# Three rows of an expert pair side by side for each partition

## The chip, the cores and the metric

The kernel runs on one core of a Trainium2 chip. The metric is the device time of one execution in microseconds; a kernel is judged by the median of several runs. The engines of the core are TensorE (PE), VectorE (DVE), ScalarE (ACT), GpSimd (POOL) and SyncE (SP, which here only issues DMAs). Each works through its own instructions in the order in which they stand, and waits on semaphores where an instruction needs another engine's or a DMA's result.

## The reference, cut to what matters

Four blocks of attention and feed-forward are applied to 4 x 256 tokens of width 256. Only the last feed-forward matters for the change: a mixture of 64 experts, of which each token takes eight. Its router and experts compute

```python
h = layernorm(x)                                  # 1024 tokens, width 256
logits = h @ gate_w                               # 64 experts
w, e = top_8(softmax(logits))                     # eight choices a token, weights summing to 1
y[token] = sum_j w[token, j] * ((silu(h @ gate_proj[e_j]) * (h @ up_proj[e_j])) @ down_proj[e_j])
x = x + y                                         # inner width of an expert: 96
```

## The kernel before

**The layers before the experts** are written as generators (`layers`, from line 450). Each step yields an `Op` with its engine, a cost in us, and what it reads and writes; a small planner (`Flow.run`) picks at every moment the request that can start first by these declared costs, with a due time as a tie-breaker, and so fixes the order of the instructions on each engine at build time. The costs that a step declares thus move the steps of other threads, too. There are two versions of the layers, for two kinds of token ids; this input takes the one built with `nk = 1`.

**Tiles.** The 1024 tokens are eight tiles of 128, one token a partition. `tile3` (line 1611) ends the last attention for one tile. Its `ps_y` (line 1623, PE) is the output projection; `add_to_x` (line 927, DVE) adds it to the tile's x. What `ps_y` needs is made by `heads3` (line 1594): exponentials on ACT (line 1566), transposes `tp_e` on PE (line 1588) with copies on ACT (line 1590), products `ps_u` on PE (line 1604) with copies to `u` on ACT (line 1608). Then the tile is routed: logits `ps_l` on PE (line 1644), the eight best on DVE (lines 1646 to 1648), and `ps_pos` on PE (line 1652), which counts for each token and expert how many tokens before it chose that expert. From this count, `pos`, DVE makes the place of each choice (lines 1657 to 1663) in `slots`.

**Places.** Each expert has room for `CAP = 192` rows; `hs` in HBM has 64 x 192 rows of 257 words: 256 of the normalized token, and one with the number of the row of `yd` to which the result belongs. Expert e's row number `pos` lies at 192 e + pos. The table `first` holds 12288 - 192 e; `first - pos` is taken so that the largest value is the first place, `ok` is 0 where the expert is full or not chosen.

**Scatter.** `normed_rows` (line 1671) makes eight copies of a tile's normalized rows in `hx`: POOL raises the variance to its power (line 1684), ACT writes the copies in two activations (line 1689). `scatter` (line 1696) sends one choice j of a tile at a time to `hs`: an indirect DMA that POOL issues (line 1702), 64 in all.

**Loads of rows.** `fill_rows` (line 441) loads the 384 rows of a pair of experts into a tile of 128 partitions x 3 x 257 words. Row number r of the pair goes to partition r mod 128, block j = r div 128, so each of the 384 runs is 1028 bytes long. SP issues these loads (line 443); the first three are issued in the layers. A load waits for the puts that can hold rows of its pair: pair 0 for choices 0 and 1 of all tiles, pair 1 for choices 0 to 3, pair 3 and later ones for all.

**Experts.** `experts` (line 2040) goes through 32 pairs in an order written out by hand. `rows_turned` (line 1887) transposes the six 128x128 blocks of a pair (`tp_hb`, PE), ACT copies them to `hbT`; then gate and up products (`ps_gu` line 2055, `ps_u` line 1986), their product on DVE (lines 1991 and 2071), and the down products `ps_y` (lines 1999 and 2004). ACT copies `ps_y` over the pair's rows (line 2083), and `put_results` (line 2007) scatters the three blocks j = 0, 2, 1 to `yd` by the row numbers in word 257. `beside` issues later loads: rows seven pairs ahead, weights, and from pair to pair the finished results of a choice (line 1927). At the end `sums` adds the weighted results to x and stores.

In the columns of `hbT`, block j and partition p stand at column 128 j + p; the first expert of a pair owns columns 0 to 191, the second 192 to 383.

Of the kernel before, what the change touches and what calls it, by code (L numbers as in the profile page):

```python
# [23 lines left out]
I32 = mybir.dt.int32  # L24
AF = mybir.ActivationFunctionType
ALU = mybir.AluOpType
AX = mybir.AxisListType

P = 128
# [17 lines left out]
E3, I3, K3 = 64, 96, 8  # L47
# [9 lines left out]
CAP = 192  # L57
HALF = P // 2
RPP = 2 * CAP // P
NROWS = E3 * CAP  # L60
# [12 lines left out]
PE, DVE, ACT, POOL, SP = "PE", "DVE", "ACT", "POOL", "SP"  # L73
# [43 lines left out]
class Flow:  # L117
# [22 lines left out]
    def go(self, gen, due=0.0):  # L140
        th = Thread(gen, due)
        self.threads.append(th)
        self.resume(th, None)
        return th
# [10 lines left out]
    def release(self, *bufs):  # L155

        for b in bufs:
            self.roles[b.role][b.slot] = max(b.used, b.ready or 0.0)
# [76 lines left out]
def model(ctx: ExitStack, tc: tile.TileContext, a: dict, out: bass.AP):  # L235
    nc = tc.nc
    PSUM = bass.MemoryType.PSUM

    const = ctx.enter_context(tc.tile_pool(name="const", bufs=1))
# [8 lines left out]
    def scal(n, name):  # L248
        return small.tile([P, n], F32, tag=f"s{n}", name=name)

    def held(pool, shape, name, dtype=F32):
        return pool.tile(shape, dtype, tag=name, name=name)
# [4 lines left out]
    def x_t(t):  # L257
        return xb[t // 2][:, t % 2, :]
# [20 lines left out]
    hs = dram.tile([NROWS, HW], F32, tag="hs", name="hs")  # L279
# [43 lines left out]
        channel_multiplier=-1,  # L323
    )
    onesb = held(const, [P, P], "onesb", BF16)
    nc.gpsimd.memset(onesb, 1.0)
    first_i = held(const, [P, E3], "first_i", I32)
    nc.gpsimd.iota(first_i, pattern=[[-CAP, E3]], base=NROWS, channel_multiplier=0)
    first = held(const, [P, E3], "first")
    nc.vector.tensor_copy(first, first_i)  # L330
    sel = held(const, [P, NT, E3], "sel", BF16)
    lgs = q1_both.rearrange("p k i -> p (k i)")[:, 2 * RPP * HW : 2 * RPP * HW + 2 * NT * E3]
    lgs = lgs.bitcast(F32).rearrange("p (t e) -> p t e", t=NT)
# [32 lines left out]
    ps = banks.tile([P, 2, NT], F32, tag="bank0", name="ps_far")  # L366
# [54 lines left out]
    def needs(ld, group, wanted, reason):  # L421

        for w in wanted:
            tc.add_manual_dep(
                ld.ins, w.name,
                mybir.DependencyInfo(mybir.DependencyClass.Sync, mybir.DependencyReason.DATA),
                reason=reason,
            )
        tc.declare_no_dep(ld.ins, group=group, keep=wanted + readers, reason=reason)
        tc.add_to_no_dep_group(group, ld.ins)  # L430
        readers.append(ld.ins)

    hbs = {
        p: v[:, : 2 * RPP * HW].bitcast(F32).rearrange("p (j d) -> p j d", j=RPP)
        for p, v in enumerate(
            (q2[2], q1_both.rearrange("p k i -> p (k i)"), q12, wmask.rearrange("p t s -> p (t s)"))
        )
    }
    in_early = len(hbs)

    def fill_rows(p, since):

        ld = nc.sync.dma_start(
            hbs[p], hs[2 * p * CAP : 2 * (p + 1) * CAP, :].rearrange("(j p) d -> p j d", p=P)
        )
        wanted = [i for n, js in zip(since, puts[: 2 * p + 2]) for i in js[n:]]
        needs(ld, "put", wanted, "rows of these choices alone")
        tc.add_to_no_dep_group("rows", ld.ins)

    def layers(nk):  # L450
# [4 lines left out]
        def due(b, stage):  # L455
            return DUE[stage] + SKEW * b
# [26 lines left out]
        def bank(shape, name):  # L483
            return ("bank", shape, name)

        def a2(shape, name, dtype=F32):
            return ("a2", shape, name, dtype)

        def a4(shape, name):
            return ("a4", shape, name)  # L490
# [17 lines left out]
        SEL = [Buf() for _ in range(NT)]  # L508
# [416 lines left out]
        def add_to_x(t, y, ps):  # L925
            yield Op(DVE, 0.39, (ps,), (X[t],))
            nc.vector.tensor_add(x_t(t), y, x_t(t))
# [428 lines left out]
        def first_rows():  # L1356
            for p in range(in_early - 1):
                yield Op(SP, 0.06, PUT[2 * p : 2 * p + 2], kb=386)
                fill_rows(p, before)
# [234 lines left out]
        def heads3(t, m, q, u):  # L1594


            n, b, es = 4 // nk, t // 2, [None, None]
            first = m * n // 4 * 8 + m * n % 4
            at = due(b, "h3") + 15.0 * (t % 2) + 3.0 * n / 2 * m
            yield Join([go(softmax3(t, first + 4 * i, q, es, i), at + 3.0 * i) for i in range(2)])  # L1600
            o = yield Op(PE, 1.25, (*es, KEYS3[b]), new=[bank([P, n, P], "ps_u3")])
            for kc in range(nk):
                for r, e in zip((lower, upper), es):
                    nc.tensor.matmul(
                        o[r], kvc[:, 2 * b + kc, :], e[:, :, kc, :], start=kc == 0, stop=kc == nk - 1
                    )
            yield Op(ACT, 0.1 + 0.4 / nk, (o,), (u,))
            nc.scalar.copy(u[:, m * n : (m + 1) * n, :], o.ap)  # L1608
            release(o, *es)

        def tile3(t, q, lane, left):

            bo3 = loads["bo3"].ap[:, : H3 // 2 * D].rearrange("p (h e) -> p h e", h=H3 // 2)
            u = yield Op(None, 0.0, new=[a4([P, H3 // 2, P], "u")])
            yield Join([go(heads3(t, m, q, u), due(t // 2, "h3")) for m in range(H3 // 8 * nk)])
            at = due(t // 2, "t3") + 15.0 * (t % 2)
            yield at
            left[0] -= 1
            if not left[0]:
                release(*q, lane)  # L1620
            y = yield Op(PE, 3.5, (u, BO3), new=[bank([P, D], "ps_y")])
            for hp in range(H3 // 2):
                nc.tensor.matmul(  # L1623
                    y.ap, u[:, hp, :], bo3[:, hp, :], start=hp == 0, stop=hp == H3 // 2 - 1
                )
            yield from add_to_x(t, y.ap, y)
            release(y, u)
            hx, w = yield Op(None, 0.0, new=[("hx", "hx"), a2([P, 2 * D], "w")])
            rows = hx.ap.rearrange("p (j d) -> p j d", j=K3)
            row_data = [Buf(), Buf()]  # L1630


            go(normed_rows(t, hx, rows, row_data), at)
            hT, rest = w[:, :D].rearrange("p (c r) -> p c r", c=2), w[:, D : D + E3]
            ok, v, top = w[:, D + E3 : D + 2 * E3], order[:, t, :], tops[:, t, :]
            tp = yield Op(PE, 0.27, (X[t],), new=[bank([P, 2, P], "tp_h")])
            for dc in range(2):
                nc.tensor.transpose(tp.ap[:, dc, :], x_t(t)[:, dc * P : (dc + 1) * P], ident)
            yield Op(ACT, 0.32, (tp,), (w,))
            nc.scalar.copy(hT, tp.ap)  # L1640
            release(tp)
            lps = yield Op(PE, 0.45, (w, GATE3C), new=[bank([P, E3], "ps_l")])
            for dc in range(2):
                nc.tensor.matmul(lps.ap, hT[:, dc, :], gate3[:, dc, :], start=dc == 0, stop=dc == 1)
            yield Op(DVE, 0.75, (lps,), (SEL[t],))
            nc.vector.max(top[:, :K3], lps.ap)
            nc.vector.match_replace(rest, top[:, :K3], lps.ap, -3.0e38)
            nc.vector.tensor_tensor(sel[:, t, :], rest, lps.ap, ALU.not_equal)

            ps = yield Op(PE, 0.06 * (t + 1), SEL[: t + 1], new=[bank([P, E3], "ps_pos")])  # L1650
            for u in range(t + 1):
                nc.tensor.matmul(
                    ps.ap, onesb if u < t else tri, sel[:, u, :], start=u == 0, stop=u == t
                )
            pos, places = ps.ap, Buf()
            yield Op(DVE, 0.85, (ps, SEL[t]), (places,))
            nc.vector.scalar_tensor_tensor(ok, pos, float(CAP), sel[:, t, :], ALU.is_lt, ALU.mult)

            nc.vector.tensor_sub(v, first, pos)
            nc.vector.tensor_mul(v, v, ok)  # L1660
            nc.vector.max(top[:, K3:], v)
            nc.vector.tensor_scalar(
                slots[:, t, :], top[:, K3:], -1.0, float(NROWS), ALU.mult, ALU.add
            )
            release(ps)
            go(scatter(t, hx, rows, row_data, places, at + 100.0), at + 100.0)
            yield Op(ACT, 0.2, (lps,), (w,))
            nc.scalar.copy(lgs[:, t, :], lps.ap)
            release(lps, w)
# [56 lines left out]
        with tc.manual_schedule(engines=ORDERED | {mybir.EngineType.SP}):  # L1726
# [5 lines left out]
            w = DUE_WEIGHTS  # L1732
# [29 lines left out]
    def ps_acc(shape, name):  # L1762
        return psum.tile(shape, F32, tag="acc", name=name, bufs=2)
# [42 lines left out]
    with tc.manual_schedule(engines=ORDERED):  # L1806
# [4 lines left out]
        ps = ps_acc([P, NT], "ps_over")  # L1811
# [14 lines left out]
    with tc.If(rv > 0):  # L1826
# [13 lines left out]
        with tc.For_i(0, E3, 1) as e:  # L1840
# [4 lines left out]
            for c in range(NCH):  # L1845
# [10 lines left out]
                for k in range(TPC):  # L1856
                    t = c * TPC + k
                    y = ps_acc([P, D], "ps_y")
                    nc.tensor.matmul(y, g[:, k * P : (k + 1) * P], dn, start=True, stop=True)
                    w = scal(1, "w_left")  # L1860
# [100 lines left out]
    rest = (slice(P, CAP), slice(0, HALF))  # L1961
# [251 lines left out]
```

## Time and profile before

| What | Value |
|---|---|
| median of 8 runs | 642.53 us (640.48 to 643.85) |
| profiled execution | 641.7 us |
| its span, first to last instruction | 639.3 us |
| mean granted TensorE clock | 0.976 |
| PE busy | 587.0 us (92%) |
| DVE, ACT, POOL busy | 423.4, 373.5, 403.7 us |
| DMA packets | 66304, 98.12 MB |
| loads of rows (line 443) | 32, 385.5 KB each |
| scatter to hs (line 1702), mean of one | 1026 ns |
| scatter to yd (line 2009), mean of one | 1001 ns |

A row of the profile names an engine, a line of the kernel and an operation; `out<-in` are the program's tiles. In brackets stands how long the engine had been idle before it and what ended that. Times of rows are us from the start of the span. The busy time of PE is modelled, and some records can be missing.

### The profile page before, as it was taken

The numbers are of one execution on the slowest core, as the hardware profiler recorded it, in microseconds if no ns is written. First come the engines' busy times: TensorE is split into PE (matmuls) and PEld (weight loads), VectorE is DVE, ScalarE is ACT, GpSimd is POOL, SyncE is SP. The second block draws the span as 40 slices with busy tenths as digits, with TensorE's granted clock in tenths as the row PEclk, the third lists the DMA queues.
The fourth block names the chain that finished last, engine by engine and source line by source line (L and its number), as shares of the span: only waits on it lengthen the run. The fifth ranks groups of instructions, "written<-read, shape, count | busy, mean of one in ns | idle before, by whom it ended". The sixth has DMA issues, their size and how long they took to land. (4 is left out here: it accounts for less than half of the span.)

```text
span 639.3 us, 10891 instructions
## 1 busy us (share of the span) xinstructions
PE 587.0 (92%) x3727; PEld 448.2 (70%) x3740; DVE 423.4 (66%) x1063; ACT 373.5 (58%) x900; POOL 403.7 (63%) x532
## 2 busy tenths in 40 slices
PE   5997799998999999999999989999739999999995
PEld 4774357686688777877876866886527887788773
DVE  5679947777687779659988767475534555434437
ACT  2233337868988976456786778579444544445420
POOL 6998898122627553564735886787773777676670
PEclk9998989998999999999999999999959999999999
DMA  8999999520200023000003111053458978978688
GB/s 297 364 387 253 219 223 252 171 58 15 83 33 3 1 67 116 2 0 1 1 2 99 42 67 58 34 190 109 158 161 265 307 238 276 302 232 305 218 261 269
DMA packets 66304, 98.12 MB, mean 153 GB/s; under 512 B 7206, under 2 KB 54007, under 8 KB 66240
## 3 DMA queue, kind: packets, MB, share of 16 engines
q1 hardware_dynamic: 56320, 78.40, 41.8%
q0 software_dynamic: 7680, 16.84, 7.4%
q10 hardware_dynamic: 2240, 2.10, 1.0%
q8 instruction: 31, 0.51, 0.4%
q14 instruction: 33, 0.27, 0.1%
HBM read 58.42 MB, written 43.07 MB: 159 GB/s over the span
## 5 line engine op out<-in xcount | busy, mean ns | idle before, releaser
L2009 POOL DMA_INDIRECT yd<-hb x84 | 84.1, 1001 | 34.2 <-issue 20.4
L1702 POOL DMA_INDIRECT hs<-hx,slots x64 | 65.7, 1026 | 24.3 <-issue 12.9
L903 POOL TENSOR_TENSOR st<-st,mhalf 128x1 f32<-128x1 f32 x56 | 32.9, 591 | 57.4 <-DVE st L899 43.1
L1566 ACT ACTIVATE e<-ps_s,nm 128x128 f32<-128x128 f32 x128 | 45.9, 421 | 5.7 <-DVE nm L1560 5.6
L1991 DVE TENSOR_TENSOR act<-ps_u,g 64x192 f32<-64x192 f32 x64 | 22.7, 354 | 39.5 <-PE ps_u L1986 39.1
L2083 ACT COPY hb<-ps_y 128x768 f32<-128x768 f32 x27 | 21.6, 800 | 36.5 <-PE ps_y L2004 36.5
L2071 DVE TENSOR_TENSOR act<-ps_gu,g 32x384 f32<-32x384 f32 x32 | 18.0, 561 | 34.2 <-ACT g L2059 33.9
L1478 POOL TENSOR_TENSOR hh<-g,v 128x512 f32<-128x512 f32 x16 | 20.2, 1274 | 23.8 <-ACT g L1476 20.0
L1281 ACT ACTIVATE qT<-tp_q,rnd 128x512 bf16<-128x512 f32 (+2 forms) x48 | 25.7, 567 | 12.2 <-PE tp_q L1277 12.2
L1566 ACT ACTIVATION_READ_ACCUMULATOR e<-ps_s,nm 128x1 f32 x128 | 32.3, 260 | 0.0
L1533 POOL TENSOR_TENSOR deep<-rt 64x512 f32<-64x512 f32 x20 | 27.1, 1355 | 5.6 <-DVE rt L1529 2.7
L1519 PE MATMUL ps_q<-qc,deep 96*128 96x256 f32 x128 | 30.4, 380 | 0.0
L906 DVE TENSOR_SCALAR h<-x,st 128x256 f32<-128x256 f32 x56 | 26.7, 489 | 5.1 <-POOL st L903 4.8
L1185 ACT ACTIVATE e<-ps_s,nb 128x256 f32<-128x256 f32 x64 | 30.1, 493 | 0.0
L1623 PE MATMUL ps_y<-bo,u 128*128 128x256 f32 x128 | 29.3, 381 | 0.1
L2059 ACT ACTIVATE g<-ps_gu 96x384 f32<-96x384 f32 x32 | 15.6, 486 | 23.2 <-PE ps_gu L2055 23.2
L1900 ACT COPY hbT<-tp_hb 128x768 f32<-128x768 f32 x31 | 24.7, 798 | 7.1 <-PE tp_hb L1892 7.1
L1120 PE MATMUL ps_g<-hT,w_gate 128*128 128x512 bf16 x69 | 20.1, 431 | 7.7 <-ACT hT L1100 4.3
L1529 DVE TENSOR_TENSOR rt<-ps_q,rope 128x512 f32<-128x512 f32 x32 | 20.9, 684 | 9.4 <-PE ps_q L1519 9.4
L1583 DVE TENSOR_TENSOR e<-e,nm 128x512 f32<-128x512 f32 x32 | 25.8, 806 | 1.3
L1519 PEld LDWEIGHTS ps_q<-qc,deep 96*128 96x128 f32 x128 | 24.1, 190 | 3.5 <-ACT qc L1505 0.3
L1623 PEld LDWEIGHTS ps_y<-bo,u 128*128 128x128 f32 x128 | 23.6, 190 | 3.4 <-ACT u L1608 0.5
(373 smaller groups left out, 1773.0 us busy)
## 6 DMA issues: line engine op xcount, KB each, us to landing
hs<-order SPq DMA_DIRECT2D x1, 12336.0 KB, 86.3
hb<-hs SPq DMA_DIRECT2D x28, 385.5 KB, 5.2
yd<-order SPq DMA_DIRECT2D x1, 8192.0 KB, 29.5
deep<-in_w_gu SPq DMA_DIRECT2D x8, 768.0 KB, 7.0
wt<-in_w_gu SPq DMA_DIRECT2D x6, 768.0 KB, 5.7
deep<-in_w_dn SPq DMA_DIRECT2D x8, 384.0 KB, 6.3
wt<-yd SPq DMA_DIRECT2D x3, 1024.0 KB, 5.5
wt<-in_w_dn SPq DMA_DIRECT2D x6, 384.0 KB, 10.5
```

Of the source, the lines that this page charges most:

```text
L903: nc.gpsimd.tensor_tensor(s[:, 8:9], s[:, 7:8], mhalf, ALU.pow)
L906: nc.vector.tensor_scalar(h[:, k, :], x_t(t), ss[k][:, 6:7], ss[k][:, 8:9], ALU.subtract, ALU.mult)
L1185: nc.scalar.activation(e[:, mt, :], s[:, mt, :], AF.Exp, bias=nb[:, mt : mt + 1], accum_out=tot[:, 2 * j + mt : 2 * j + mt + 1],)
L1281: nc.scalar.activation(qT[:, 4 * i : 4 * i + full, :], tp.ap[:, :full, :], AF.Identity, bias=rnd[:, 1:2])
L1519: nc.tensor.matmul(ps.ap[:, k, :], w[:, hp * P : (hp + 1) * P], qc.ap, start=True, stop=True)
L1533: nc.gpsimd.tensor_add(qv(q[i])[r, hps, :], t0[r], t1[r])
L1566: nc.scalar.activation(wide[:, k, :], s.ap[:, k, :], AF.Exp, bias=nm[:, k : k + 1], accum_out=tot[:, k : k + 1],)
L1583: nc.vector.tensor_mul(wide, wide, tot.unsqueeze(2).to_broadcast([P, n, nk * P]))
L1623: nc.tensor.matmul(y.ap, u[:, hp, :], bo3[:, hp, :], start=hp == 0, stop=hp == H3 // 2 - 1)
L1702: put = nc.gpsimd.indirect_dma_start(out=hs[:, :], out_offset=bass.IndirectOffsetOnAxis(ap=slots[:, t, j : j + 1], axis=0), in_=rows[:, j, ...
L1900: copied = nc.scalar.copy(hbT, tp[:, :, : RPP * P])
L2009: put = nc.gpsimd.indirect_dma_start(out=yd[:, :], out_offset=bass.IndirectOffsetOnAxis(ap=hbs[p][:, j, D : D + 1].bitcast(I32), axis=0), ...
```

## The change

A pair's rows are placed differently. For position `pos` of a token in its expert, the first expert of a pair takes row 3 pos of the pair, the second row 3 pos + 2; a position from 128 on is bent back to the middle rows: the first expert's 128 to 191 go to rows 1, 4, ..., the second's to the middle rows of partitions 64 to 127. Partition p then holds rows 3p, 3p + 1 and 3p + 2, which lie side by side in `hs`, so a load is 128 runs of 3084 bytes. The columns of `hbT` belong to the same experts as before. In block j = 1, which before held the first 64 rows of the second expert and the first expert's rows past 128, now only rows past 128 of either expert lie; block j = 2 holds the second expert's first 128.

The table `first` gets a second half, `back_to`, made by a second iota and one wider cast. Two DVE operations are added for each tile, and the step declares 1.1 us in place of 0.85, and that it writes the tile's scratch `w`.

```diff
-    first_i = held(const, [P, E3], "first_i", I32)
-    nc.gpsimd.iota(first_i, pattern=[[-CAP, E3]], base=NROWS, channel_multiplier=0)
-    first = held(const, [P, E3], "first")
-    nc.vector.tensor_copy(first, first_i)
+    first_i = held(const, [P, 2, E3], "first_i", I32)
+    nc.gpsimd.iota(
+        first_i[:, 0, :], pattern=[[-2 * CAP, E3 // 2], [1 - RPP, 2]], base=NROWS, channel_multiplier=0
+    )
+    nc.gpsimd.iota(
+        first_i[:, 1, :], pattern=[[0, E3 // 2], [2 - RPP * HALF, 2]], base=RPP * P - 1,
+        channel_multiplier=0,
+    )
+    firsts = held(const, [P, 2, E3], "first")
+    nc.vector.tensor_copy(firsts, first_i)
+    first, back_to = firsts[:, 0, :], firsts[:, 1, :]
...
-            hbs[p], hs[2 * p * CAP : 2 * (p + 1) * CAP, :].rearrange("(j p) d -> p j d", p=P)
+            hbs[p], hs[2 * p * CAP : 2 * (p + 1) * CAP, :].rearrange("(p j) d -> p j d", p=P)
...
-            yield Op(DVE, 0.85, (ps, SEL[t]), (places,))
+            yield Op(DVE, 1.1, (ps, SEL[t]), (places, w))
             nc.vector.scalar_tensor_tensor(ok, pos, float(CAP), sel[:, t, :], ALU.is_lt, ALU.mult)
 
-            nc.vector.tensor_sub(v, first, pos)
+            nc.vector.scalar_tensor_tensor(rest, pos, float(P), back_to, ALU.is_ge, ALU.mult)
+            nc.vector.scalar_tensor_tensor(v, pos, float(-RPP), first, ALU.mult, ALU.add)
+            nc.vector.tensor_add(v, v, rest)
             nc.vector.tensor_mul(v, v, ok)
```

The order of the instructions before the experts changes with it on PE, DVE, ACT and POOL, from the routing of the first tile on; the orders of SP and of the expert stage are the same as before.

## Prediction

> **What bounds the kernel now.** I read the table of stages first, because the page's shares (PE 92% busy) mix stages with different limits. Its columns are start:end, length, then busy us (and instructions) of PE, PE's weight loads, DVE, ACT and POOL, then granted clock, DMA share, GB/s.
>
> ```profile
> 405.00:425.00 20.00, 20.00 (x135) 17.64 (x134) 13.86 (x37) 11.56 (x36) 15.39 (x20) 1.00 0.21 71
> 460.00:470.00 10.00, 1.61 (x14) 1.27 (x14) 3.71 (x15) 3.49 (x8) 8.13 (x18) 0.64 0.26 88
> 470.00:476.00 6.00, 1.59 (x7) 1.22 (x7) 2.75 (x7) 2.24 (x4) 5.02 (x10) 0.50 0.68 167
> 476.00:484.00 8.00, 6.78 (x34) 5.42 (x35) 1.73 (x4) 2.64 (x4) 2.02 (x3) 0.76 0.56 164
> 484.00:612.00 128.00, 128.00 (x903) 101.81 (x900) 60.62 (x146) 62.83 (x91) 88.69 (x88) 1.00 0.83 272
> 622.00:640.00 18.00, 9.95 (x38) 6.20 (x36) 13.18 (x32) 0.00 (x0) 0.36 (x2) 1.00 0.79 266
> ```
>
> The reader is to see that the expert stage (484 to 612) has PE busy for all of its 128 us, while the layers before it keep PE nearly full, and that only the passage between them, 460 to 484, leaves PE idle. There POOL is the busy engine, with the last scatters. So a row load that lands sooner is worth something in the passage and nothing inside the expert stage. The chain of waits names POOL there, but POOL only follows PE's 4.25 us per pair (its puts begin at 491.94, 496.19 and so on).
>
> Second, who waits for the row loads of line 443, asked by source line (time and count; then landing in us, least, median, most):
>
> ```profile
>   PE tp_hb L1892: 6.9, 2
>   PEld tp_hb L1892: 0.7, 1
> ...
> DMA to landing us min/median/max: 3.2/5.2/14.8
> ```
>
> Of 32 loads only the first two are waited for: 14.8 us in flight hurts nobody, since loads are issued seven pairs ahead.
>
> Third, the passage in order of time:
>
> ```profile
> 461.82 0.59 POOL L1684 TENSOR_TENSOR rstds<-st,mhalf 128x1 f32<-128x1 f32 x1
> 467.20 0.97 POOL L1702 DMA_INDIRECT hs<-hx,slots  x1 [0.22 <-issue]
> 469.89 6.04 SPq L443 DMA_DIRECT2D q<-hs  x3
> 473.84 1.51 PE L1892 MATMUL tp_hb<-ident,q 128*128 128x128 f32 x6 [6.53 <-DMA q<-hs]
> 480.45 0.87 PE L1892 MATMUL tp_hb<-ident,q 128*128 128x128 f32 x6 [0.33 <-DMA q<-hs]
> ```
>
> The last tile's scale is made at 461.82; four puts follow at 1.28 us each, the fourth (tile 7, choice 1, at 467.20) ends what pair 0 waits for; its load goes out at 469.89, is used at 473.84, and the second pair's transposes wait 0.33 us more for their load.
>
> **The change part by part.**
>
> *Two added DVE operations per tile.* The operations at lines 1657 and 1659 take 217 to 226 and 209 to 213 ns and start up to 0.26 us apart; 16 more make 16 x 0.26 = 4.2 us of DVE over 350 to 463. DVE is busy 13.86 of 20 us there, so the sum is hidden; on a path lies only the last tile's 0.5 us. It is covered too: before, that tile's slots end at 463.24 (463.07 + 0.17), and its first put starts at 465.93, behind two puts of tile 6. Cover 2.7 us, cost 0; 0.5 us if the cover is gone. The second iota and the longer cast run in the first 6 us (186 ns each before): 0, at most 0.4.
>
> *The planner's order.* The declared 1.1 in place of 0.85 us and the added write of w move instructions on PE, ACT, DVE and POOL from tile 0's slots on; on SP nothing moves. I followed the end of both orders. What decides is the time from tile 6's update of x to tile 7's:
>
> ```profile
> 451.60 0.42 DVE L927 TENSOR_TENSOR x<-ps_y,x 128x256 f32<-128x256 f32 x1 [0.29 <-PE ps_y L1623]
> 453.94 2.37 ACT L1689 ACTIVATE hx<-x,st,rstds 128x1024 f32<-128x1024 f32 x2 [0.37 <-POOL tick L1701]
> 456.32 0.58 ACT L1608 COPY u<-ps_u 128x512 f32<-128x512 f32 x1
> 458.98 0.42 DVE L927 TENSOR_TENSOR x<-ps_y,x 128x256 f32<-128x256 f32 x1 [2.85 <-PE ps_y L1623]
> ```
>
> Before, 7.38 us (451.60 to 458.98): ACT makes both copies of tp_e (452.09 and 452.99) ahead of the hx pair, so PE's last ps_u runs at 453.59 and ps_y of tile 7 at 454.85. In the new order the hx pair stands ahead of both copies, and ps_u waits for them: 2.34 (451.60 to the hx pair's start) + 2.37 (the pair) + 1.07 (two copies, 0.49 apart, the second 0.58) + 1.08 (ps_u, row at 438.12; 1.11 at 453.59) + 3.62 (a ps_y undisturbed, row at 447.94) = 10.48. That is 3.1 later, counted from tile 6. Against it, one ps_u pass (1.08) that stood ahead of tile 6's ps_y now stands behind it, so tile 6 may be up to 1.08 earlier if PE sets that stretch, and not at all if ACT does, as between 425 and 440 (14.69 of 15 us busy). I take half: 0.5. Net **+2.6** at tile 7. POOL passes it on: two puts of tile 6 and two of tile 7 stand between the scale and what pair 0 waits for, in both orders (choices 4 and 5 of tile 6 before, 5 and 6 after). Behind them come seven puts instead of eight; that 1.28 us is off the path, as pair 3's rows land at 485.96 and are used at 487.71. The whole order since 350 us is shuffled, with PE waits of only about 5 us there in all, so this term may be anything from -1.1 to +5.
>
> *The row loads.* 384 runs of 1028 bytes become 128 of 3084. The trace's packet records have 1028-byte packets at a mean of 80 ns in the first load, 64 in the next two and 58 in 520 to 560 (median 47); the nearest long ones, 512 packets of 3072 bytes at the start, at 128 (median 124). In the DMA view of 469.9 to 474.1:
>
> ```profile
> q1 hardware_dynamic: 400, 0.39, 46.2%
> q0 software_dynamic: 166, 0.49, 30.8%
> ```
>
> The first load's packets fill 384 x 80 / 16 = 1.93 us of sixteen queues, and would fill 128 x 128 / 16 = 1.02: 0.9 us sooner. By medians it is 384 x 47 / 16 = 1.13 against 0.99, so 0.1. The rest of its 3.95 us until use is latency. The second load must also come sooner to keep the gain, and it was used 0.33 us late already. I take **-0.6**, between 0 and -0.9; the value lies nearer the first because the same two streams, puts and loads, meet here again. In the expert stage each load frees (384 x 58 - 128 x 128) / 16 = 0.37 us of DMA time per 4.25 us pair: 0, hidden behind PE's 128 of 128 us; without that cover it would still be no more than 32 x 0.37 = 12.
>
> [...]
>
> *The scatters and the results.* Still 64 puts into hs (mean 1026 ns) and 96 into yd (1001 ns), with the same number of live rows; POOL's time did not depend on how many rows were live (0.97 in nearly every row), so 0. The wait for the last put changes a little: choice block j=1, put last, held 64 rows of the odd expert and now holds the overflow past row 128 alone.
>
> ```profile
> 621.31 3.58 DMA yd<-hb
> 625.93 7.47 DMA ctxT<-yd
> ```
>
> An unloaded put lands in 2.4 us (row at 606.78) against 3.58 + 0.12 here, but the put ahead of it, at 620.03, now carries more rows, and the four 512 KB loads behind fill the queues (share 0.79 over the tail). I take **-0.3**, between 0 and -1.3.
>
> **Sum.** +2.6 - 0.6 - 0.3 = +1.7. The profiled execution took 641.7 (span 639.3 and 2.4 around it), so 643.4; it lies 0.8 below the median of 642.53, so the median goes to **644.2**. About 0.2%, or 1.3 us, is what measurement can tell from no change.
>
> **Rivals.**
> *The order pays off.* Tile 6 takes the full 1.08, and enough of the hx pair's wait falls on work that PE has anyway that tile 7 is also 1.1 early. Then -1.1 - 0.9 - 0.3 = -2.3: 640.2. For it: PE waited only 3.0 us for ACT's copies at line 1590 between 340 and 460, and both orders hold the same work. Against it: the ACT order above is fixed, in-order and counted. It decides once tile 7's update comes at least 0.4 us early (-0.4 - 0.6 - 0.3 = -1.3). Chance 0.27.
> *Even.* The order costs about 1 us and the loads and tail return it: 642.6. Chance 0.22.
> *No help from longer runs.* Landing is latency and one slow queue (the second and third loads' last packets trail to 481.2), the order costs its full 3.1 and the slots' 0.5 is uncovered: +3.6, 646.1. Chance 0.15.
> *The change not doing what it says* is unlikely: the compiled loads read 128x771 in place of 128x3x257. It would be the case above.
> My forecast, slower by 1.3 to 3, keeps 0.36. So faster 0.27, same 0.22, slower 0.36 + 0.15 = 0.51. The range, **640.6 to 647.2**, takes in the first rival nearly to its value and the last with 1 us of shuffle beyond it. Slower alone would be 643.8 to 647.2.
>
> **What would show it.** Right: packets fall by 32 x 256 = 8192 from 66304; PE stays at 128 of 128 us in the expert stage; tile 7's update comes over 9 us after tile 6's, the last scale at about 464.4, pair 0's load out near 472.5, its transposes near 475.8. Wrong: a last scale at or before 461.8 (the order term), a first load not landing sooner than 3.9 us after issue (the load term), or an expert stage with a period other than 4.25 us.

## The result and the profile after

The changed kernel takes 648.70 us (median of 17 runs, 646.77 to 650.76) against 642.64 us for the kernel before on the same chip (46 runs): ratio 1.0099, 95% interval 1.0087 to 1.0111, so 6.1 us slower. The forecast was 644.2 with a range to 647.2: the right side, but outside the range. The profiled execution of the changed kernel took 650.47 us (span 648.7), 1.8 above its median, where that of before was 0.9 below its own; so the two profiles differ by 8.8 us where the medians differ by 6.1. This matters for the tail, below.

The table of stages again (start:end, length; busy us of PE, PE's weight loads, DVE, ACT and POOL; granted clock, DMA share, GB/s), with the stages about 7 us later:

```profile
405.00:425.00 20.00, 17.63 (x110) 14.37 (x109) 15.48 (x29) 11.57 (x51) 14.75 (x17) 1.00 0.36 125
467.00:477.00 10.00, 2.05 (x16) 1.47 (x16) 5.07 (x20) 3.92 (x8) 7.60 (x15) 0.67 0.26 86
477.00:483.00 6.00, 1.91 (x7) 1.54 (x8) 2.96 (x7) 2.19 (x3) 4.83 (x10) 0.50 0.68 175
491.00:619.00 128.00, 128.00 (x902) 101.62 (x902) 60.87 (x146) 62.58 (x91) 88.69 (x88) 1.00 0.81 268
629.00:648.00 19.00, 12.04 (x37) 8.19 (x35) 13.22 (x32) 0.00 (x0) 0.09 (x2) 0.82 0.76 263
```

The expert stage is as it was: PE busy for 128 of 128 us, a pair every 4.25 us. What is new stands ahead of it: from 405 to 425 PE now stands idle for 2.4 of 20 us, where it was full. The passage in order of time shows the same chain as before, later:

```profile
468.39 0.57 POOL L1693 TENSOR_TENSOR rstds<-st,mhalf 128x1 f32<-128x1 f32 x1 [0.73 <-DVE st L1690]
474.97 1.32 POOL L1711 DMA_INDIRECT hs<-hx,slots  x1 [0.23 <-issue]
476.98 5.55 SPq L450 DMA_DIRECT2D q<-hs  x3
480.52 1.51 PE L1901 MATMUL tp_hb<-ident,q 128*128 128x128 f32 x6 [4.96 <-DMA q<-hs]
486.94 1.13 PE L1901 MATMUL tp_hb<-ident,q 128*128 128x128 f32 x6
```

The last scale is 6.6 us later (468.39 for 461.82), pair 0's load 7.1 (476.98 for 469.89), its first use 6.7 (480.52 for 473.84); the second pair no longer waits for its load. From issue to use the first load takes 3.54 us where it took 3.95. The loads by source line, and the transfers while the first load is under way:

```profile
  PE tp_hb L1901: 5.0, 1
...
DMA to landing us min/median/max: 2.8/4.9/14.9
```

```profile
q1 hardware_dynamic: 144, 0.39, 42.1%
q0 software_dynamic: 173, 0.47, 30.3%
```

Packets fall from 66304 to 58112, by the 8192 forecast, and 400 packets of q1 become 144. But their time on the queues hardly falls (42.1% of a window of 4.2 us, for 46.2%). Last, the stretch from tile 6's update of x to tile 7's:

```profile
455.31 0.42 DVE L934 TENSOR_TENSOR x<-ps_y,x 128x256 f32<-128x256 f32 x1
457.65 2.37 ACT L1698 ACTIVATE hx<-x,st,rstds 128x1024 f32<-128x1024 f32 x2 [0.44 <-POOL tick L1710]
459.93 1.04 ACT L1597 COPY e<-tp_e 128x512 f32<-128x512 f32 x2
460.55 2.45 PE L1611 MATMUL ps_u<-e,kvc 128*64 128x512 f32 x4 [1.46 <-ACT e L1597]
462.93 4.04 PE L1630 MATMUL ps_y<-bo,u 128*128 128x256 f32 x16
467.01 0.42 DVE L934 TENSOR_TENSOR x<-ps_y,x 128x256 f32<-128x256 f32 x1 [6.40 <-PE ps_y L1630]
```

It is as the forecast read it off the two orders, the hx pair ahead of the copies and ps_u waiting for them, but 11.7 us long (10.48 forecast, 7.38 before); and tile 6 itself comes at 455.31, 3.7 us later than before, where the forecast had it 0.5 sooner. Together tile 7 is 8.0 us late. How PE spent the time from 340 us, where both kernels still have the same order and the changed one is 0.4 us late in this execution, to the updates of tile 6 and of tile 7; first before, then after, with one stretch more:

```profile
340.00:451.60 111.60, 106.48 (x649) 84.57 (x648) 74.46 (x194) 82.97 (x277) 83.57 (x135) 1.00 0.28 92
340.00:459.00 119.00, 113.57 (x688) 89.18 (x686) 77.39 (x207) 87.36 (x284) 88.59 (x145) 1.00 0.30 98
```

```profile
340.00:455.30 115.30, 106.81 (x648) 84.23 (x649) 78.11 (x206) 83.16 (x277) 85.16 (x138) 1.00 0.29 98
340.00:467.00 127.00, 116.22 (x691) 89.92 (x690) 81.39 (x221) 88.04 (x285) 91.94 (x153) 0.99 0.28 95
460.55:462.93 2.38, 2.38 (x5) 0.58 (x5) 0.05 (x1) 0.54 (x2) 1.35 (x3) 0.50 0.00 0
```

Idle time of PE is length less busy: 5.4 us before, 10.8 after. So of the 8.0 us, 5.35 are idle time and 2.65 are busy time. By tile 6's update the idle time is 8.5 us for 5.1: 3.4 of the 3.7 us that tile 6 is late. It was added between 380 and 437 us (5.0 us for 1.2), though tile 5's update at the end of that stretch is still on time (438.19 for 438.43). Behind tile 6 the clock plays a part: it was 0.50 from 460.55 to 462.93, while ps_u ran, and stood at 1.00 there before (453 to 459). The last ps_u took 2.45 us for 1.11 before, the last ps_y 4.04 us for the 3.62 of an undisturbed one. In the waits of PE from 340 us on no single one stands out, before and then after (total, times, longest):

```profile
PE ps_u L1604 <- ACT e L1590: 3.0, 2, 2.2
PE ps_qc L1500 <- ACT hT L922: 1.0, 2, 0.7
```

```profile
PE ps_u L1611 <- ACT e L1597: 4.9, 4, 1.6
PE tp_e L1595 <- DVE e L1590: 2.2, 4, 1.1
PE ps_pos L1659 <- DVE sel L1655: 1.0, 2, 0.8
```

### The profile page after: what moved, and what is told of

It is laid out like the page before. It is cut to its first block, busy times and chain, and to the rows that moved or that the text cites. A ratio compares the mean times of both kernels' runs of the same rounds, so it can differ in the third digit from the quotient of the medians.

```text
span 648.7 us, 10911 instructions
## 1 busy us (share of the span) xinstructions
PE 592.3 (91%) x3727; PEld 451.1 (70%) x3740; DVE 428.8 (66%) x1079; ACT 373.9 (58%) x900; POOL 404.4 (62%) x533
## 2 busy tenths in 40 slices
DMA packets 58112, 98.12 MB, mean 151 GB/s; under 512 B 7206, under 2 KB 41719, under 8 KB 58048
## 4 chain that ended last, share of the span: by engine, by line
PE 45%; POOL 14%; DVE 12%; ACT 12%; issue 11%; DMA 5%; POOLq 1%; DVEq 0%; ACTq 0%; SPq 0%
POOL yd L2018 10%; PE ps_q L1526 6%; PE ps_g L1127 3%; ACT e L1573 2%; PE ps_y L1630 2%; DMA yd<-hb 2%; PE ps_u L1127 2%; PE ps_y L1409 2%; PE tp_q L1284 2%; PE ps_u L1611 2%; PE ps_s L1387 2%; PE ps_p L749 2%; ACT hx L1698 1%; PE ps_p L945 1%; PE tp_e L1200 1%
## 5 line engine op out<-in xcount | busy, mean ns | idle before, releaser
L1711 POOL DMA_INDIRECT hs<-hx,slots x64 | 65.1, 1018 | 25.4 <-issue 11.5
L910 POOL TENSOR_TENSOR st<-st,mhalf 128x1 f32<-128x1 f32 x56 | 32.8, 590 | 57.0 <-DVE st L906 44.8
```

What stands on the lines that cost most here:

```text
L910: nc.gpsimd.tensor_tensor(s[:, 8:9], s[:, 7:8], mhalf, ALU.pow)
L1711: put = nc.gpsimd.indirect_dma_start(out=hs[:, :], out_offset=bass.IndirectOffsetOnAxis(ap=slots[:, t, j : j + 1], axis=0), in_=rows[:, j, ...
```

## The experiments

Theory: the time comes from the order that the planner writes out for the new declaration. Rivals: the added operations or the new layout cost it; or, within the order, one place alone (tile 6's hx pair). The kernels ran in five groups, each on one chip beside the kernel before. In the first three groups that kernel took 682.0, 674.6 and 682.7 us, in the last two 642.9 and 642.1; so only ratios to the kernel before within a group are compared, and moments only within a group, or between the last two groups and the first measurement.

### First group: which part of the change

The four corners: layout old or new, declaration old or new, and the declaration's two halves.

```diff
 e1, in the changed kernel:
-            yield Op(DVE, 1.1, (ps, SEL[t]), (places, w))
+            yield Op(DVE, 0.85, (ps, SEL[t]), (places,))
 e2, in the kernel before:
-            yield Op(DVE, 0.85, (ps, SEL[t]), (places,))
+            yield Op(DVE, 1.1, (ps, SEL[t]), (places, w))
 e3, in the changed kernel: Op(DVE, 1.1, (ps, SEL[t]), (places,))
 e4, in the changed kernel: Op(DVE, 0.85, (ps, SEL[t]), (places, w))
```

> The changed kernel with the routing step declared as before (0.85 us, without the write of w): same instruction order as before, new places, new loads and the two added DVE operations kept. Theory 'order' (the loss is the planner's new order; it measured +8.0 us at the last tile's update of x): tile 7's update comes within 1 us of 459.0, pair 0's transposes start at about 473.3 (the shorter load gives 0.4 back), and the time is 641.5 to 643, equal to before within 0.2%. Theory 'layout' (the two operations and the new places cost it): still 646 or more.

> The kernel before with only the declaration changed (1.1 us and the write of w): the changed kernel's instruction order, with the old places, the 1028-byte runs and no added operation. Theory 'order': slower by 5.5 to 7.5 us, 648 to 650, tile 7's update at 466 to 467. Theory 'layout': equal to before within 0.2%.

> The changed kernel with 1.1 us declared, but without the write of w: a third order. Theory 'order' in the form that any shuffle of an order costs: slower than before by 2 to 8 us. In the form that only this one order is bad (the hx pair ahead of two copies on ACT, near its end): within 2 us of before, and the distance from tile 6's to tile 7's update of x says which: 7.4 us where the copies go first, over 10 where they do not. Theory 'layout': 646 or more whatever the order.

> The changed kernel with 0.85 us declared and the write of w: a fourth order. Theory 'order': its time follows tile 7's update of x one for one (time = 642.5 + that update's time - 459.0, within 1.5 us), whatever its sign. Theory 'layout': 646 or more whatever the order.

Measured, as ratio to before with its 95% interval: e1 1.0006 (0.9977 to 1.0034), e2 1.0070 (1.0031 to 1.0108), e3 1.0102 (1.0047 to 1.0156), e4 1.0035 (1.0009 to 1.0061). With the old declaration the new layout and the added operations cost nothing that can be measured here; with the new declaration the old layout is slower by 0.7%, which its interval does not tell from the changed kernel's 1.0%. In the profiles e2's tile 7 is 8.6 us later than e1's (486.0 for 477.4) and its first transposes 7.0 (500.0 for 493.0), and its span is 6.9 longer. The order is the cause. Each half of the declaration gives another order: e3's time can't be told from e2's, and e4's lies between e1's and theirs, with an interval that overlaps both. The rule that e4 was to test, the time following tile 7's update one for one, did not hold: e4's tile 7 is 4.3 us after e1's and its median 1.7, e2's 8.6 and 5.2.

### Second group: which order, and which place in it

```diff
 e5, in the changed kernel, ahead of the hx activations:
+            if t == 6:
+                yield due(3, "t3") + 40.0
 e6: Op(DVE, 0.95, (ps, SEL[t]), (places,))
 e7: Op(DVE, 1.0, (ps, SEL[t]), (places, w))
 e8: e1 again
```

> The changed kernel, with one exchange on ACT and nothing else moved on PE, DVE or POOL in the branch that runs: the two hx activations of tile 6 stand behind the two copies of tp_e again. Theory 'one stretch' (the forecast's: the added time comes from the stretch between the x updates of tiles 6 and 7, where ps_u waits for the hx pair): tile 7's update comes 2.4 us sooner, the two updates stand 9.3 us apart, the time is 646.3 us, 1.006 of the kernel before. Theory 'many gaps' (PE stands still a little in some ten places of 340 to 467, and this is one of them): tile 7's update gains no more than the gap at this place, 1.46 us, the two stand 10.2 us apart or more, the time is 647.2 or later, at or above 1.0073, and the remaining 5 to 6 us stay.

> The changed kernel with 0.95 us declared for the slots on DVE in place of 1.1 (with or without the write of w the order comes out the same): the planner writes out a third order. Theory 'any other order costs' (the order of before is a lucky one, and the order that follows from any other declared cost leaves PE more idle): PE's idle time between 340 us and tile 7's update is above 8 us against 5.4 before, and the time is 1.004 of before or more. Rival 'the 1.1 order is a bad one by itself': a cost close to the old one gives a time within 0.3% of before. Rival 'the layout or the two operations cost': it stays at 1.007 or more whatever the order.

> The changed kernel with 1.0 us declared and the write of w kept: a fourth order. Theory 'any other order costs': 1.004 of before or more, with more than 8 us of PE idle between 340 us and tile 7's update. Rival 'the 1.1 order is a bad one by itself': within 0.3% of before, or faster. In both, the end follows the first transposes of the expert stage by about 165.5 to 168 us, so the time can be read off the moment of the first tp_hb.

> The changed layout and the added operations in the old order (0.85 us declared, places alone written), once more, beside the kernels with other orders and with five rounds, to bound what layout and operations do by themselves. By the forecast's terms: loads -0.6, tail -0.3, operations 0, so 0.9986 of before (-0.9 us). By 'the tail pays' (in the changed kernel's profile the last transposes stand 34.5 us from the end, before 31.8): +0.9 to +2.7 us, 1.0015 to 1.004. By 'operations cost 0.5 at the last tile': 0 to +0.5 with the loads' gain, 1.000.

(What e6 says in brackets does not hold: with the write of w the order at 0.95 is another, which was not run. In e5 the pair came to stand between the two copies, not behind both.)

Measured: e5 1.0102 (1.0066 to 1.0138), e6 0.9996 (0.9971 to 1.0021), e7 1.0018 (0.9991 to 1.0044), e8 1.0028 (1.0004 to 1.0053). So it is not so that any other order costs: those of 0.95 and 1.0 measure within 0.2% of the kernel before, and their first transposes come at 489.1 and 489.8, where e8 has 489.4 and e5 496.1. The orders of 1.1 us are bad by themselves. (From the first transposes to the end it is 183.6 to 185.4 us in these four, not the 165.5 to 168 that e7 names.) e8 is the kernel of e1, which measured 1.0006 on another chip; here its interval lies just above 1, where "the tail pays" had it, so a cost of layout and operations of up to 0.5% on this chip is not excluded. In e5 the two updates stand 10.0 us apart, but tile 6 comes at 472.1, 5.7 us later than in e8: most of the loss stands ahead of the place that the forecast named. Its interval is too wide to say whether the exchange gave back 1.5 us.

### Third group: early or late tiles, and an order that seemed better

```diff
 e9 and e10, in the changed kernel:
-            yield Op(DVE, 1.1, (ps, SEL[t]), (places, w))
+            new = t < 4          # e10: t >= 2
+            yield Op(DVE, 1.1 if new else 0.85, (ps, SEL[t]), (places, w) if new else (places,))
 e11, in the kernel before: Op(DVE, 0.95, (ps, SEL[t]), (places,))
 e12: e6 again
```

> The changed kernel with the new declaration (1.1 us and the write of w) for the slots of tiles 0 to 3 alone, the old one for tiles 4 to 7: in the branch that runs, PE, DVE and POOL keep exactly the changed kernel's order, ACT differs in a few copies. Theory 'upstream' (the loss is made by PE's order from about 350 us on, which the first tiles' declaration sets, and tile 6 is late already): the time is 1.007 to 1.010 of before, and tile 6's update of x comes 3 us or more later than in the old order on the same chip. Forecast's theory (tile 6's own hx pair ahead of the copies, tile 6 no later): tile 6 within 1 us of the old order, and the loss, if any, all behind it.

> The changed kernel with the new declaration for tiles 2 to 7 alone, the old one for tiles 0 and 1: PE and DVE keep exactly the old order, on ACT only the small copies of ps_l stand one or two places elsewhere. Theory 'upstream': 1.000 of before, at most 1.003. Rival 'the price of the late tiles' slots counts' (a wait for w or a later place that the longer declaration asks for by itself): 1.004 or more.

> The kernel before, old layout and no added operations, with 0.95 us declared: the order on PE and ACT is that of the changed layout with 0.95 us (the next kernel), so the two differ in layout and added operations alone. Theory 'order': within 0.3% of before, as the changed layout was with this order. Rival 'old layout gains by this order what the new one then loses': 0.997 of before or less.

> The changed layout and operations with 0.95 us declared, beside the old layout in the same order on the same chip. By the forecast's terms (loads -0.6, tail -0.3, operations 0) 0.9 us less than its neighbour; the load of pair 0 is used 0.4 to 0.6 us sooner after its issue. By 'the tail pays': 1 to 3 us more than its neighbour, and seen between the last transposes and the end. By 'the operations cost 0.5 at the last tile': 0 to 0.5 more.

Measured: e9 1.0076 (1.0034 to 1.0118), e10 0.9982 (0.9957 to 1.0006), e11 0.9946 (0.9923 to 0.9968), e12 0.9992 (0.9969 to 1.0014). With the new declaration for the first tiles alone PE's order is the changed kernel's, the time can't be told from it, and tile 6 is at 476.9 where e10, with PE's old order, has 466.5. With the new declaration for tiles 2 to 7 PE's order stays, and so does the time. "Upstream" stood the test; the price of the late tiles did not. The pair e11 and e12 was a surprise: one order, yet the new layout 3.2 us slower, and e11 faster than before. Hence the next group.

### Fourth group: operations and layout by themselves

```diff
 e13: e11 again
 e14: e11 with
+            nc.vector.scalar_tensor_tensor(rest, pos, float(P), first, ALU.is_ge, ALU.mult)
             nc.vector.tensor_sub(v, first, pos)
+            nc.vector.tensor_add(rest, v, rest)
 e15: e6 again
```

> The old layout with 0.95 us declared, on another chip, beside the next two, which have its order exactly on PE and ACT. Theory 'this order is better than the old one': 0.9946 of before again, at most 0.998. Rival 'no better, the 3.7 us belonged to that chip': 0.998 to 1.002.

> The kernel of e13 with the two added DVE operations of the same shapes (64 columns, one of them read from PSUM), their result used by nothing: old layout, same order, so the difference to e13 is the price of the operations alone. Forecast: 0 (cover 2.7 us at the last tile), at most 0.5 us. Rival 'the operations cost': 8 tiles of about 0.4 to 0.5 us on the way from ps_pos to the scatters, 1 to 3 us if they push the puts of every tile.

> The changed layout with its operations in the same order: the difference to e14 is the price of the layout alone, scatter places and loads. Forecast: -0.9 us. Rival 'the layout costs' (on the chip of e11 and e12 layout and operations cost 3.2 us together, seen between the first transposes and the end): +1 to +3 us here too, seen there again. If e13 to e15 are within 1.5 us of one another, the 3.2 us were that chip's or chance.

Measured: e13 1.0000 (0.9978 to 1.0022), e14 0.9989 (0.9971 to 1.0006), e15 0.9986 (0.9970 to 1.0002). On this chip, which runs the kernel before as the first one did, the operations cost nothing that can be measured, the layout neither costs nor gains (medians 642.46 and 642.32 us), and the order of 0.95 us is as good as the old one and not better. So the whole change but its declaration is within 0.3% of the kernel before here. The 3.2 us of e11 and e12 did not come again on this chip; what they were is open. No version was shown to beat the kernel before on both chips that it ran on: e11 was 0.5% faster, e13, the same kernel, was not.

### Fifth group: ACT's order or PE's

```diff
 e16: the changed kernel
 e17, ahead of the hx activations:
+            if t in (2, 6):
+                yield due(t // 2, "t3") + 15.0 * (t % 2) + (45.0 if t == 2 else 40.0)
 e18: 50.0 in place of 45.0
```

> The changed kernel itself, so that the next two have it beside them on the same chip. All theories: 1.007 to 1.011 of before.

> The changed kernel with two exchanges on ACT alone, at the two places where its trace has PE waiting for a copy of tp_e that stands behind a pair of hx activations (1.62 us at tile 2's pair, 1.46 us at tile 6's): the first copy of tp_e, at tile 2 the second too, comes ahead. PE, DVE and POOL keep the changed kernel's order. Theory 'hx ahead of copies on ACT is the loss': 3 us back or more, 1.004 of before or less. Theory 'PE's order is the loss': at most the two gaps come back, no more than 2 us, and as much as none of it: 1.006 or more.

> The same with tile 2's pair put off 5 us further, from which the planner writes out another order on PE as well (42 places differ from the changed kernel's). Theory 'PE's order is the loss': the time moves away from the changed kernel's by more than 2 us, with PE's idle time between 340 us and tile 7's update, and it follows the moment of the first tp_hb as in all runs so far. Theory 'hx ahead of copies on ACT': as e17.

Measured: e16 1.0104 (1.0075 to 1.0133), e17 1.0081 (1.0053 to 1.0109), e18 1.0161 (1.0133 to 1.0189); medians 649.46, 647.42 and 652.79 us. The waits for ACT's copies from 385 to 465 in e16, then in e17:

```profile
PE ps_u L1611 <- ACT e L1597: 3.6, 3, 1.6
PE tp_e L1595 <- DVE e L1590: 2.3, 3, 1.1
```

```profile
PE tp_e L1595 <- DVE e L1590: 2.6, 3, 1.1
PE ps_u L1611 <- ACT e L1597: 1.6, 3, 0.6
```

and the end of e17's stretch, to be held against the changed kernel's above:

```profile
456.85 2.37 ACT L1700 ACTIVATE hx<-x,st,rstds 128x1024 f32<-128x1024 f32 x2
459.75 1.07 PE L1611 MATMUL ps_u<-e,kvc 128*64 128x512 f32 x2 [0.45 <-ACT e L1597]
460.75 3.72 PE L1630 MATMUL ps_y<-bo,u 128*128 128x256 f32 x16
464.51 0.42 DVE L934 TENSOR_TENSOR x<-ps_y,x 128x256 f32<-128x256 f32 x1 [4.71 <-PE ps_y L1630]
```

The two exchanges took 2.0 us of waiting off ps_u, and the median is 2.0 us lower, though the intervals overlap. But tile 6 comes at 454.5 in e17 and at 454.6 in e16: the 1.1 us saved at tile 2's pair are waited for elsewhere before tile 6. All that is gained is gained behind it (tile 7 at 464.5 for 466.3). About 1.0 us of this is ps_u's wait at that place (0.45 us for 1.46). The rest goes with the clock: e16's was 0.50 from 459.5 to 462.9, as in the changed kernel, e17's 1.00 from 454.5 to 464.5, and its ps_y runs 3.72 us in place of 4.08. By the medians ACT's pairs are some 30% of the loss, an estimate; most of it, 1.0081, stays with PE's order untouched. In e18, with PE's order changed too, PE waits at other places and longer:

```profile
PE ps_u L1611 <- ACT e L1597: 4.3, 1, 4.3
PE tp_e L1595 <- ACT e L1597: 3.5, 1, 3.5
```

PE's idle time from 340 us to tile 7's update (its records, as above) against the ratio, over all kernels profiled on chips of this speed:

| kernel | tile 6, tile 7 (us) | PE idle (us) | first transposes | ratio |
|---|---|---|---|---|
| before | 451.6, 459.0 | 5.4 | 473.8 | 1 |
| e15 | 450.5, 458.0 | 6.4 | 472.1 | 0.9986 |
| e14 | 450.8, 458.3 | 6.4 | 472.6 | 0.9989 |
| e13 | 454.1, 461.6 | 7.7 | 475.5 | 1.0000 |
| e17 | 454.5, 464.5 | 9.1 | 477.8 | 1.0081 |
| e16 | 454.6, 466.3 | 10.4 | 479.9 | 1.0104 |
| changed | 455.3, 467.0 | 10.8 | 480.5 | 1.0099 |
| e18 | 454.3, 469.7 | 14.0 | 483.3 | 1.0161 |

The time follows PE's idle time ahead of tile 7's update, whatever the layout, between the harmless orders (up to 7.7 us) and the bad ones (from 9.1). Each row is one execution: e13, e14 and e15 have one order on PE and ACT and stand 1.3 us apart, so smaller differences say nothing.

What stays open: which exchange in PE's order makes tile 6 late. One candidate was read off the traces: in the changed kernel ACT stands idle for 6.9 us behind PE's ps_q block, with five groups of ps_s in one burst behind it, where before it was 4.5 us. But e7, whose profile has 8.0 us there, cost 0.2%, and e18, with 5.0, cost 1.6%; so that idle time by itself does not decide.

## Why the prediction was right and wrong

**The order term is the step that failed**: +2.6 forecast (-1.1 to +5), +7.1 measured at pair 0's load. The mechanism was the right one (e1 against e2), and the named stretch was there; the sizes were off in two places. First, "I take half: 0.5", tile 6 sooner, was +3.7: the forecast read the two orders closely behind tile 6 only and settled everything ahead of it by the one pass of ps_u seen to change sides. The order differs from 350 us on (on PE from 366), and PE's idle time ahead of tile 6 grew by 3.4 us. Second, the stretch of 10.48 was 11.7: the one pass of ps_u behind the copies stood where it was forecast, but the sum took its price, and ps_y's, at full clock. The clock was 0.50 from 460.55 to 462.93; copies and ps_u took 3.0 us together (459.93 to 462.93) for 2.15, and ps_y 4.04 for 3.62. Against it went 0.9 us behind tile 7: the scale followed its update by 1.4 us for 2.8, and the load the scale by 8.6 for 8.1.

**The bound of the range failed with it.** "PE waits of only 5 us in all" was taken as a measure of what a shuffle can do. It is how much the old order had left to lose, not what a new one can add: 10.8 us in the changed kernel, 14.0 in e18.

**Row loads**: -0.6 forecast, -0.4 measured from issue to use (3.95 to 3.54), and 3.75 to 3.66 between e14 and e15. The term was small either way, but its working was wrong. The packet records have the 3084-byte packets of the first load at a mean of 221 ns (median 122), not 128: together 1.77 us of sixteen queues, for 1.93 before; in e14 and e15 it is 1.57 and 1.63. The 3072-byte packets whose 128 ns it borrowed had run at the start, with no puts beside them (from 8.3 to 14.2 us, where q0, the queue of the puts, moved no packet); with puts under way the time on the queues fell by 0.16 us, not by the 0.9 of the means.

**Operations** 0, **scatters** 0, **expert stage** unchanged: right. e14 shows the first, the puts' mean of 1018 ns (1026) the second, 128 of 128 us the third.

**Tail**: -0.3 forecast, because the last put, with fewer rows, would land sooner. It lands later. The last put of the changed kernel, then of e15 (new layout) and e14 (old layout), which share one order:

```profile
628.05 6.15 DMA yd<-hb
619.18 5.96 DMA yd<-hb
619.95 3.50 DMA yd<-hb
```

In the three old layouts profiled on chips of this speed it took 3.48 to 3.58 us, in the five new ones 5.71 to 6.94. The loads of results behind it are shorter in return: the one that is waited for took 4.10 to 5.38 us there and 6.92 to 7.47 in the old layout. What is left of it is hard to see beside the clock. From the last transposes to the end, in the kernel before, the changed one, e13 (old layout) and e15 (new):

```profile
607.50:639.30 31.80, 23.62 (x115) 16.60 (x113) 17.68 (x46) 4.00 (x7) 11.08 (x13) 1.00 0.81 266
614.30:648.70 34.40, 25.91 (x115) 18.77 (x112) 17.72 (x46) 3.94 (x7) 11.01 (x13) 0.89 0.75 247
609.40:643.70 34.30, 25.58 (x115) 18.65 (x113) 17.68 (x46) 4.02 (x7) 11.09 (x13) 0.90 0.74 247
605.40:638.20 32.80, 23.86 (x115) 16.49 (x113) 17.73 (x46) 3.97 (x7) 11.06 (x13) 1.00 0.80 258
```

A clock of 0.89 or 0.90 goes with a longer tail, in the old layout as in the new. At 1.00 the new layout's took 32.8 us, the old one's 31.8 and, in e14, 31.1: 1.0 to 1.7 us more, where 0.3 less was forecast, in one execution each. The medians of e14 and e15 don't show it, so what the tail is worth in the time stays open.

**The rivals.** "The order pays off" and "even" fell with the scale at 468.39. "No help from longer runs" came nearest (646.1): right that longer runs bring little, but it still priced the order at 3.1 and made up the rest with 0.5 for the operations, which cost nothing. The signs to look for held where they concerned the mechanism (packets, 128 of 128, over 9 us between the two updates) and failed where they gave moments (464.4, 472.5, 475.8 for 468.4, 477.0, 480.5).

## What to carry to other kernels

A cost or a write that is declared to a list scheduler is part of the kernel: here 0.25 us and one more written buffer in a declaration, for operations that themselves cost nothing, moved four engines' orders for 100 us and cost 1%. After such an edit, hold the declaration fixed, measure the edit, and then treat each declared value as a kernel of its own: 0.95 and 1.0 us were harmless, 1.1 was not, nor, in a smaller measure, 0.85 with the write of w (1.0035). When two orders must be compared on paper, go through the bounding engine's waits from the first instruction that moved, not from the last tile back; and take the idle time of the old order for what it can lose, not for what a new one can add.

## What the hardware showed that was not expected

- A packet three times as long took 2.7 times as long when puts ran beside it: 1028 bytes at a mean of 81 ns in the first load before, 3084 bytes at 221 ns after; in 40 us of the expert stage 58 ns and 161 ns. Medians were 47 and 122 ns. A third of the packets saved 9% of the time on the queues there (11.5 us of sixteen queues for 12.6), not two thirds.
- In the tail the granted clock fell to 0.5 for 3.4 to 6.8 us in some executions and not in others, with either layout. The tail took 31.1 to 32.8 us without and 33.2 to 34.9 with. In the two profiles, before and after, the only granted clocks are 1.00 and 0.50, and the stretches at 0.50 that end within the span last 3.41, 6.83 or 17.07 us. What decides whether a tail dips is not shown by a run here.
- One such stretch, of 3.4 us, stands between tile 6 and tile 7 in the changed kernel, e16 and e18, right where PE waits for the copies, and in none of before, e14, e15 and e17; e13 has one ahead of tile 6 (446.5 to 449.9). What falls into it runs at half the clock: a matmul record of ps_u took 1.12 us there and 0.64 elsewhere. That the wait brings on the stretch is not shown.
- The same kernel took 642 us on some chips and 675 to 683 on others. There the time from the first transposes to the last was 149 to 156 us for 134, and in most of the kernels ACT stood still once between 430 and 470 us for some 5 to 10 us with DVE idle beside it (ACT 8.0 and DVE 11.9 in e1), though not in e4 and e7. The cause is open; the order's price was nearly the same there (0.7 to 1.0%).
